# Alternating high and low weight blocks on TensorE, and a router issued in two steps

## The chip, the cores and the metric

The kernel runs on one core of a Trainium2 chip. The metric is the device time of one execution in microseconds. The engines are named as the profile names them: PE (TensorE matmuls), PEld (TensorE weight loads), DVE (VectorE), ACT (ScalarE), POOL (GpSimd), SP (SyncE, which issues most DMAs).

## The reference

Eight sequences of 256 tokens with 1024 features pass through four layers; each layer adds its result to its input. All matrices are 1024 x 1024, and all data are fp32.

```
x = x + L0(x)   # x @ W.T  +  2 * mixture of 8 rank-16 adapters; per token a router picks
                # the top 2 of 8 logits (5.0 is added to one expert per sequence) and
                # weighs them by a softmax over the two
x = x + L1(x)   # x @ W.T + b + coeff[b] * (x @ (2 * mask[b] - 1)),  mask int32, per sequence
x = x + L2(x)   # x @ weight[id[b]].T,  one of 8 full matrices per sequence
x = x + L3(x)   # rank-16 adapter id[b]:  (x @ B[id].T) @ A[id].T
```

## The kernel before

**Precision.** TensorE multiplies fp32r data. A value is split in a high part (a cast to fp32r on ACT) and a low part (the value less its high part, a subtraction on DVE), and a product is taken as high x high + high x low + low x high, in one PSUM accumulator.

**Stages.** The eight sequences are four pairs q, worked on in two halves g of two pairs each. A half is: layer 0 for both its pairs, then layers 1 and 2 of its first pair, then of its second. The work is cut into slots. A half has 16 slots of layer 0 (called s = 0 to 15, with a Strassen-like scheme of seven block products) and 4 x 16 slots of layers 1 and 2.

**Layers 1 and 2.** A slot is one block of 128 output features (m) for one sequence (j): eight k-blocks of weights, each 128 x 128. The activations lie as [k, j, high/low, 256 tokens], so one matmul of the high weight block against 512 columns gives high x high in the first 256 columns and high x low in the last 256; a second matmul of the low weight block against the 256 high columns is added onto the first half. Function `two` (L519) does this: eight high matmuls (L524), then eight low ones (L533). The last slot of all uses `three` instead. `evacuate` later adds the two halves with bias and the residual: ACT copies one half, DVE adds the other.

**Work between the matmuls.** `two` takes three lists of further PE work: `early` runs after the second high matmul, `mid` between the high and the low run, `late` at the end. `main` fills them: layer 3's projections, the rank step and its final matmuls (`proj_pair`, `rank_pair`, `finish` at L463, called through `fill`), and, before the second half begins, the logits of its router.

**Preparation.** ACT casts the high block of the item four ahead (`highs`, L288, five buffers); DVE subtracts for the low block of the item up to three ahead (`lows`, four buffers; line 68 is the helper through which all DVE tensor-tensor operations go). The table `LAGS` delays some of these subtractions around the change from layer 1 to layer 2. Everything is issued in an order written out by hand; each engine works through its own queue in that order.

**Layer 0.** A slot issues, in this order: copies of finished accumulators out of PSUM (`l0_evacuate`, among them L734 in slot 6), casts and subtractions for later slots, the works listed for the slot by `l0_works`, and then the PE work of `l0_main`. The router of a pair runs as such a work: `logits` (L308) and `by_token` (transposes, L319) on PE, then `router` (L323) with some twenty small DVE operations that end in `d`, the difference of the two best logits, an exponential `ex` on ACT (L357), and six small DVE operations that give the two weights; then `expand` (L371) spreads them to `gx`. `gates_by_rank` transposes `gx` on PE (L385) in the middle of a later slot: in slot 3 for the first pair and in slot 6 for the second. In slot 5 the first pair's gates, split into `ghi` and `glo`, enter the products of `lora` (L622) as high x high, high x low and low x high.

In the first half `l0_works` places the router like this:

```
at(2, *both(less, "T1", 1, 0), lambda: router([p0]), lambda: expand(p0))
at(5, lambda: router([p1]), lambda: expand(p1))
```

The second half's router runs for both pairs at once, in the last slot of the first half.

Of the kernel before, what the change touches and what calls it, by code (L numbers as in the profile page):

```python
# [8 lines left out]
F32 = mybir.dt.float32  # L9
# [6 lines left out]
P = 128  # L16
# [3 lines left out]
K = 8  # L20
# [14 lines left out]
def kernel(ctx: ExitStack, tc: tile.TileContext, x, lang, coeff, ids,  # L35
# [23 lines left out]
    gp = ctx.enter_context(tc.tile_pool(name="g", bufs=1))  # L59
# [7 lines left out]
    def tt(o, a, b, op):  # L67
        nc.vector.tensor_tensor(o, a, b, op)  # L68
# [106 lines left out]
    def pair_of(g, j):  # L175
        return 2 * g + 1 - j
# [60 lines left out]
    def fold_quad(t, h, eng=None):  # L237
        for k in range(2):
            c = (2 * h + k) * P
            fold_block(t[:, k, c:c + P], eng)  # L240
# [77 lines left out]
        for n in range(4):  # L318
            nc.tensor.transpose(pts[p][:, n * P:(n + 1) * P], lg[:, n * P:(n + 1) * P], ident)  # L319

    gxs = {}

    def router(pairs):  # L323
        n4 = 4 * len(pairs)
        t = lambda nm, w: gp.tile([P, n4, w], F32, tag=nm, name=nm)
        lv = t("lv", E)
        for i, p in enumerate(pairs):
            quarters = pts.pop(p).rearrange("p (n g e) -> p n e g", n=4, g=4)[:, :, :E, :]
            nc.vector.tensor_reduce(
                lv[:, 4 * i:4 * i + 4].rearrange("p n (e o) -> p n e o", o=1), quarters, AX.X,  # L330
                ALU.add)
        b0, nb = 2 * pairs[0], 2 * len(pairs)
        lv4 = lv.rearrange("p (b h) e -> p b h e", h=2)
        tt(lv4, lv4, bias[:, b0:b0 + nb].rearrange("p b (o e) -> p b o e", o=1)
           .to_broadcast([P, nb, 2, E]), ALU.add)
        revb = rev.to_broadcast([P, n4, E])

        def top(v, nm):
            mx = t(f"mx{nm}", 1)
            nc.vector.tensor_reduce(mx, v, AX.X, ALU.max)  # L340
            eq = t(f"eq{nm}", E)
            tt(eq, v, mx.to_broadcast([P, n4, E]), ALU.is_equal)
            tt(eq, eq, revb, ALU.mult)
            fi = t(f"fi{nm}", 1)
            nc.vector.tensor_reduce(fi, eq, AX.X, ALU.max)
            oh = t(f"oh{nm}", E)
            tt(oh, revb, fi.to_broadcast([P, n4, E]), ALU.is_equal)
            return mx, oh

        m1, oh1 = top(lv, "1")  # L350
        rest = t("rest", E)
        nc.vector.scalar_tensor_tensor(rest, oh1, -3.0e38, lv, ALU.mult, ALU.add)
        m2, oh2 = top(rest, "2")
        d = t("d", 1)
        tt(d, m2, m1, ALU.subtract)
        ex = t("ex", 1)
        nc.scalar.activation(ex, d, AF.Exp)  # L357

        den = t("den", 1)
        nc.vector.tensor_scalar(den, ex, 1.0, 0.5, ALU.add, ALU.mult)  # L360
        wt1 = t("wt1", 1)
        nc.vector.reciprocal(wt1, den)
        wt2 = t("wt2", 1)
        tt(wt2, wt1, ex, ALU.mult)
        tt(oh1, oh1, wt1.to_broadcast([P, n4, E]), ALU.mult)
        tt(oh2, oh2, wt2.to_broadcast([P, n4, E]), ALU.mult)
        tt(oh1, oh1, oh2, ALU.add)
        for i, p in enumerate(pairs):
            gxs[p] = oh1[:, 4 * i:4 * i + 4, :]

    def expand(p):  # L371

        gx = gp.tile([P, 4 * E, R], F32, tag="lg", name=f"gx{p}", bufs=3)
        nc.vector.tensor_copy(gx, gxs[p].rearrange("p n (e o) -> p (n e) o", o=1)
                              .to_broadcast([P, 4 * E, R]))
        gxs[p] = gx
# [21 lines left out]
    def gate(p):  # L398
        tt(gts[p], phs.pop(p), gts[p], ALU.mult)
# [119 lines left out]
    def two(po, hi, lo, xhl, j, early=(), mid=(), late=()):  # L519


        for k in range(K):
            c = slice(k * P, (k + 1) * P)
            mm(po, hi[:, c], xhl[:, k, j].rearrange("p h t -> p (h t)"), start=(k == 0),  # L524
               stop=False)
            if k == 1:
                for f in early:
                    f()
        for f in mid:
            f()  # L530
        for k in range(K):
            c = slice(k * P, (k + 1) * P)
            mm(po[:, :T], lo[:, c], xhl[:, k, j, 0, :], start=False, stop=(k == K - 1))  # L533
        for f in late:
            f()

    def three(po, hi, lo, xhl, j):
        for k in range(K):
# [51 lines left out]
    def link(*args, **kw):  # L590

        mm(*args, skip_group_check=True, **kw)  # L592
# [29 lines left out]
    def lora(p, w):  # L622
        def part(m, o, stop=False):
            hi, lo = gates[p]
            link(o, w[0](m), hi, start=False, stop=False)
            link(o, w[0](m), lo, start=False, stop=False)
            link(o, w[1](m), hi, start=False, stop=stop)
        return part

    def lb_half(i):  # L630
# [16 lines left out]
    def sub(g, o, a, b, h):  # L647
        q = [flat(quad(g, n)[h]) for n in (o, a, b)]
        tt(q[0], q[1], q[2], ALU.subtract)
# [12 lines left out]
    def l0_works(g):  # L662


        p0, p1 = pair_of(g, 0), pair_of(g, 1)
        w = {}

        def at(s, *fs):
            w.setdefault(s, []).extend(fs)

        def add(name, h, src):
            nc.gpsimd.dma_start(quad(g, name)[h], src, accum_op=ALU.add)

        def s1_add(h):
            fold_quad(quad(g, "S1")[h], h)
            add("S1", h, w0[1, 2 + h])

        def s3_add(h):
            t = quad(g, "S3")[h]
            copy(flat(t), flat(quad(g, "S2")[h]))  # L680
            fold_quad(t, h)
            add("S3", h, w0[1, 2 + h])

        def s4_add(h):
            copy(flat(quad(g, "S4")[h]), flat(quad(g, "S2")[h]))
            add("S4", h, w0[0, 2 + h])

        def less(h, name, j, i):

            t = flat(quad(g, name)[h])  # L690
            nc.scalar.mul(t, t, -1.0)  # L691
            add(name, h, x[pair_of(g, j)][:, 4 * i + 2 * h:4 * i + 2 * h + 2])

        def both(f, *args):
            return [lambda h=h: f(h, *args) for h in range(2)]

        def subs(o, a, b):
            return [lambda h=h: sub(g, o, a, b, h) for h in range(2)]

        def lb_parts():  # L700
            copy(lbs[0], lb_raw)
            tt(lbs[1], lb_raw, f32(lbs[0]), ALU.subtract)

        if g == 0:
            at(1, constants, *both(s1_add))
            at(2, *both(less, "T1", 1, 0), lambda: router([p0]), lambda: expand(p0))
            at(3, lb_parts, *subs("S2", "A11", "S1"))
            at(4, *both(s4_add), lambda: gate(p0))
            at(5, lambda: router([p1]), lambda: expand(p1))
        else:  # L710
            at(0, *both(s1_add), *both(less, "T1", 1, 0))
            at(2, lambda: expand(p0))
            at(3, *subs("S2", "A11", "S1"))
            at(4, *both(s4_add), lambda: gate(p0))
            at(5, lambda: expand(p1))
        at(-5, lambda: split_gates(p0, gts[p0]))
        at(4, *both(less, "T3", 1, 1))
        at(7, *subs("T2", "T1", "B22"))
        at(7, *both(s3_add))
        at(8, lambda: gate(p1), lambda: split_gates(p1, gts[p1]), lambda: gate_difference(g))  # L720
        for h in range(2):
            at(9 + h, lambda h=h: add("T4", h, x[p0][:, 4 + 2 * h:6 + 2 * h]))
        for i in range(4):
            at(12 + i, lambda i=i: split_c(p1, i))
        return w
# [183 lines left out]
    def side(n):  # L909

        kind, q, m, j = slots[n]
        if kind == "L1":
            return
        u = pos[slots[n]] % 16
        b = 2 * q
        if q % 2 == 0:
            if u < 2:
                load_l3(b + u)
            if u in (4, 5):
                prep_l3(b + u - 4)  # L920
            if u in (2, 5, 8, 11):
                split_c(q + 1, u // 3)
            return
        l, p = ((9, 10), (11, 12)) if q == 1 else ((4, 5), (9, 10))
        if u in l:
            load_l3(b + u - l[0])
        if u in p:
            prep_l3(b + u - p[0])
        if q == 1:
            if u == 0:  # L930
                X[1] = region(GX[1], "x1", [P, 2, K, N], F32)
            if u in (1, 3, 5, 7):
                k = 4 * (u // 2 % 2)
                load_x(1, u // 4, k, k + 4)
            if u == 10:
                LA[1] = place_la(2)
                nc.sync.dma_start(LA[1], la)
            if u in (12, 13):
                la_parts(1, 4 * (u - 12), 4 * (u - 12) + 4)
            if u == 15:  # L940
                router([2, 3])

    def unit_slot(n):
        kind, q, m, j = slots[n]
# [56 lines left out]
    for h in range(2):  # L1001
        for k in range(2):
            m = 2 * h + k
# [29 lines left out]
    at = l3[b]  # L1033
# [9 lines left out]
    for m in range(0, half, 2):  # L1043
        po = bank(m, f"po{b}_{m}")
        for n in range(2):
            mm(po[:, n * T:(n + 1) * T], at[:, (m + n) * P:(m + n + 1) * P], rt, start=True,
               stop=True)
# [66 lines left out]
```

## Time and profile before

| | |
|---|---|
| median of 3 runs | 614.74 us (613.67 to 614.75) |
| profiled execution, its own time | 613.21 us |
| its span, first to last instruction | 611.0 us |
| mean granted TensorE clock | 0.994 |
| busy: PE, PEld, DVE | 597.0, 500.6, 474.5 us |
| busy: ACT, POOL | 385.1, 140.3 us |
| high matmuls of layers 1 and 2 (L524) | 1016, 392 ns each as recorded |
| low matmuls (L533) | 1016, 283 ns each as recorded |
| bytes moved | 130.22 MB, mean 213 GB/s |

The recorded length of a matmul contains its way through the array and overlaps with the next one; the time that a matmul takes in a row of matmuls is the distance to the next start. Layer 0 of the first half lies at 6 to 119 us, layers 1 and 2 of the first half at 119 to 307, layer 0 of the second half at 307 to 413, layers 1 and 2 of the second half at 413 to 600. Times in the text are microseconds from the span's start unless marked ns.

### The profile page before, as it was taken

How to read it: one execution, taken by the hardware profiler on the slowest of the kernel's cores; microseconds unless marked ns; L12 is line 12 of the kernel's file. 1: busy time of each engine (PE TensorE's matmuls, PEld its weight loads, DVE VectorE, ACT ScalarE, POOL GpSimd, SP SyncE). 2: the span in 40 equal slices, each digit the busy share in tenths (PEclk: the TensorE clock that was granted, in tenths of full speed). 3: DMA queues.
4: the chain of work that ended last, by engine and by line, in shares of the span. 5: the costliest groups of instructions: out<-in, count | busy, mean ns of one | idle time of the engine just before them, and what ended most of it. 6: DMA issues, size and time to landing. Idle time of an engine off the chain costs nothing.

```text
span 611.0 us, 8941 instructions
## 1 busy us (share of the span) xinstructions
PE 597.0 (98%) x3244; PEld 500.6 (82%) x3244; DVE 474.5 (78%) x555; ACT 385.1 (63%) x455; POOL 140.3 (23%) x174
## 2 busy tenths in 40 slices
PE   8997999999999999999999999999999999999995
PEld 7775788888888888888778778888888888888874
DVE  5576858899789999577656776879968999977752
ACT  4574656687678797554544746558866788864431
POOL 0320343014122213122210233511333111511000
PEclk9998999999999999999999999999999999999998
DMA  8986598267685767599940798935767686847404
GB/s 292 330 196 123 137 217 230 104 219 298 191 298 209 248 255 283 183 364 324 291 76 2 163 242 200 276 118 207 276 189 259 207 285 232 301 147 242 173 1 137
DMA packets 39389, 130.22 MB, mean 213 GB/s; under 512 B 4786, under 2 KB 6194, under 8 KB 38578
## 3 DMA queue, kind: packets, MB, share of 16 engines
q1 hardware_dynamic: 34594, 112.62, 52.6%
q0 software_dynamic: 4608, 16.78, 14.9%
q8 instruction: 25, 0.41, 0.3%
q10 hardware_dynamic: 144, 0.26, 0.1%
q14 instruction: 18, 0.15, 0.1%
HBM read 121.25 MB, written 8.39 MB: 212 GB/s over the span
## 4 chain that ended last, share of the span: by engine, by line
PE 92%; DVE 3%; ACT 2%; issue 1%; DMA 1%; ACTq 0%
PE po L524 38%; PE mm L592 27%; PE po L533 20%; PE pl L308 1%; DVE wlo L68 1%; PE pf L463 1%; PE pb L435 1%; ACT x L691 1%; PE ph L619 1%; PE ph L618 1%; PE ph L620 1%; ACT whi L288 1%; DMA x<-in_x 1%; DVE c L68 0%; PE pb L482 0%
## 5 line engine op out<-in xcount | busy, mean ns | idle before, releaser
L524 PE MATMUL po<-hl,whi 128*128 128x512 f32 x1016 | 254.5, 392 | 0.0
L524 PEld LDWEIGHTS po<-hl,whi 128*128 128x128 f32 x1016 | 182.7, 189 | 32.7
L68 DVE TENSOR_TENSOR wlo<-raw,whi 128x1024 fp32r<-128x1024 f32 x128 | 160.9, 1267 | 1.2 <-issue 1.1
L533 PEld LDWEIGHTS po<-hl,wlo 128*128 128x128 f32 x1016 | 137.6, 190 | 11.3 <-issue 1.6
L288 ACT CAST whi<-raw 128x1024 fp32r<-128x1024 f32 x128 | 133.7, 1048 | 18.0 <-PE mm L592 8.4
L533 PE MATMUL po<-hl,wlo 128*128 128x256 f32 x1016 | 142.3, 283 | 0.0
L592 PE MATMUL mm<-whi,whi 128*128 128x512 f32 x224 | 88.9, 397 | 5.1 <-ACT c L734 3.5
L592 PE MATMUL mm<-wlo,whi 128*128 128x512 f32 x224 | 88.2, 394 | 0.0
L235 POOL TENSOR_TENSOR raw<-raw,ident 128x128 f32<-128x128 f32 x72 | 59.2, 823 | 116.9 <-DMA raw<-in_w 86.9
L257 ACT ACTIVATE raw<-raw,negc,c 128x1024 f32<-128x1024 int32 x64 | 79.6, 1243 | 4.2 <-DMA raw<-in_mask 4.2
L592 PE MATMUL mm<-whi,wlo 128*128 128x512 f32 x224 | 71.7, 396 | 0.0
L235 POOL TENSOR_TENSOR w<-w,ident 128x128 f32<-128x128 f32 x28 | 34.6, 1237 | 158.3 <-DMA w<-in_w 134.1
L68 DVE TENSOR_TENSOR raw<-raw,w 128x1024 f32<-128x1024 f32 x56 | 69.3, 1237 | 1.5 <-POOL w L235 0.9
L68 DVE TENSOR_TENSOR wlo<-x,whi 128x1024 fp32r<-128x1024 f32 (+1 forms) x38 | 45.4, 1204 | 21.0 <-issue 10.3
L592 PEld LDWEIGHTS mm<-whi,whi 128*128 128x128 f32 x224 | 42.3, 189 | 17.6 <-ACT c L734 4.0
L592 PEld LDWEIGHTS mm<-whi,wlo 128*128 128x128 f32 x224 | 42.5, 190 | 9.9 <-DVE wlo L68 0.8
L592 PEld LDWEIGHTS mm<-wlo,whi 128*128 128x128 f32 x224 | 42.3, 189 | 8.7
L288 ACT CAST whi<-A 128x1024 fp32r<-128x1024 f32 x26 | 27.3, 1050 | 34.4 <-PE mm L592 16.9
L565 ACT COPY c<-po 128x512 f32<-128x512 f32 (+1 forms) x34 | 18.8, 552 | 47.0 <-PE po L533 47.0
L568 ACT ACTIVATE sum<-po,b_sb 128x512 f32<-128x512 f32 (+1 forms) x36 | 23.1, 642 | 31.6 <-PE po L533 31.6
L288 ACT CAST whi<-x 128x1024 fp32r<-128x1024 f32 x34 | 35.3, 1048 | 8.9 <-PE mm L592 8.9
L68 DVE TENSOR_TENSOR wlo<-A,whi 128x1024 fp32r<-128x1024 f32 (+1 forms) x30 | 35.8, 1193 | 4.7 <-ACT whi L827 2.7
(126 smaller groups left out, 523.6 us busy)
## 6 DMA issues: line engine op xcount, KB each, us to landing
raw<-in_mask SPq DMA_DIRECT2D x64, 512.0 KB, 5.5
raw<-in_w SPq DMA_DIRECT2D x64, 512.0 KB, 4.8
w<-in_w SPq DMA_DIRECT2D x28, 512.0 KB, 3.4
out<-c SPq DMA_DIRECT2D x31, 256.0 KB, 3.0
A<-in_w SPq DMA_DIRECT2D x14, 512.0 KB, 8.1
x<-in_x SPq DMA_DIRECT2D x6, 1024.0 KB, 7.8
A<-in_w POOLq DMA_DIRECT2D x12, 512.0 KB, 7.9
x<-in_x POOLq DMA_DIRECT2D x12, 512.0 KB, 8.5
```

The costliest lines, as they stand in the source:

```text
L68: nc.vector.tensor_tensor(o, a, b, op)
L235: (eng or nc.gpsimd).tensor_tensor(t, t, ident, ALU.add)
L257: nc.scalar.activation(f32(raws[n]), raws[n], AF.Identity, bias=negc[:, b:b + 1], scale=c2[:, b:b + 1])
L288: copy(prep_hi(i), flat(source(i)))
L308: mm(pl[c:c + 32, :], wrs[:, k, :], X[g][:, j, k, :], start=(k < 4), stop=(k >= 4))
L435: mm(pb[c:c + 32, j * T:(j + 1) * T], l3b[b][:, k, :], xts[b][:, k, :], start=(k < 4), stop=(k >= 4))
L463: mm(po[:, i * T:(i + 1) * T], at[:, (m + i) * P:(m + i + 1) * P], rt, start=True, stop=True)
L524: mm(po, hi[:, c], xhl[:, k, j].rearrange("p h t -> p (h t)"), start=(k == 0), stop=False)
L533: mm(po[:, :T], lo[:, c], xhl[:, k, j, 0, :], start=False, stop=(k == K - 1))
L565: copy(xs, po[:, :, T:])
L568: nc.scalar.activation(xs, po[:, :, T:], AF.Identity, bias=b1c)
L592: mm(*args, skip_group_check=True, **kw)
```

## The change

In `two` the low matmul of each k-block now follows the high matmul of the same block; `early` runs after the second pair, `mid` after the fourth pair, `late` after the eighth. The router is cut in two behind `d`: `router` keeps what comes before, and the new `weigh` does the exponential and the weights. In the first half `weigh` and `expand` are issued one slot later than `router`; in the second half `weigh` follows `router` at once. In `lora` the product with the gates' low part comes third instead of second.

```diff
     def router(pairs):
...
         d = t("d", 1)
         tt(d, m2, m1, ALU.subtract)
+        routed[tuple(pairs)] = d, oh1, oh2
+
+    def weigh(pairs):
+
+        n4 = 4 * len(pairs)
+        t = lambda nm, w: gp.tile([P, n4, w], F32, tag=nm, name=nm)
+        d, oh1, oh2 = routed.pop(tuple(pairs))
         ex = t("ex", 1)
         nc.scalar.activation(ex, d, AF.Exp)
...
             mm(po, hi[:, c], xhl[:, k, j].rearrange("p h t -> p (h t)"), start=(k == 0),
                stop=False)
-            if k == 1:
-                for f in early:
-                    f()
-        for f in mid:
-            f()
-        for k in range(K):
-            c = slice(k * P, (k + 1) * P)
             mm(po[:, :T], lo[:, c], xhl[:, k, j, 0, :], start=False, stop=(k == K - 1))
-        for f in late:
-            f()
+            for f in {1: early, 3: mid, K - 1: late}.get(k, ()):
+                f()
...
             link(o, w[0](m), hi, start=False, stop=False)
-            link(o, w[0](m), lo, start=False, stop=False)
-            link(o, w[1](m), hi, start=False, stop=stop)
+            link(o, w[1](m), hi, start=False, stop=False)
+            link(o, w[0](m), lo, start=False, stop=stop)
...
-            at(2, *both(less, "T1", 1, 0), lambda: router([p0]), lambda: expand(p0))
-            at(3, lb_parts, *subs("S2", "A11", "S1"))
+            at(2, *both(less, "T1", 1, 0), lambda: router([p0]))
+            at(3, lambda: weigh([p0]), lambda: expand(p0), lb_parts, *subs("S2", "A11", "S1"))
             at(4, *both(s4_add), lambda: gate(p0))
-            at(5, lambda: router([p1]), lambda: expand(p1))
+            at(5, lambda: router([p1]))
+            at(6, lambda: weigh([p1]), lambda: expand(p1))
...
             if u == 15:
                 router([2, 3])
+                weigh([2, 3])
```

More of the change, by code (lines that the diff above doesn't have):

```diff
@@ L319, in by_token @@
             nc.tensor.transpose(pts[p][:, n * P:(n + 1) * P], lg[:, n * P:(n + 1) * P], ident)
-    gxs = {}
+    gxs, routed = {}, {}
     def router(pairs):
```

## The prediction

> **What bounds the kernel now.** I read first the page's busy shares and its chain of waits, then the waits of PE, then the order of time on PE, ACT and DVE where PE stands still, and last the order of time on PE in the middle of layer 1.
>
> ```profile
> PE 597.0 (98%) x3244; PEld 500.6 (82%) x3244; DVE 474.5 (78%) x555; ACT 385.1 (63%) x455; POOL 140.3 (23%) x174
> PE 92%; DVE 3%; ACT 2%; issue 1%; DMA 1%; ACTq 0%
> PE po L524 38%; PE mm L592 27%; PE po L533 20%; PE pl L308 1%; DVE wlo L68 1%; PE pf L463 1%; PE pb L435 1%; ACT x L691 1%; PE ph L619 1%; PE ph L618 1%; PE ph L620 1%; ACT whi L288 1%; DMA x<-in_x 1%; DVE c L68 0%; PE pb L482 0%
> ```
>
> PE carries 92% of the chain, and the two lines that the change interleaves, L524 (high block) and L533 (low block), are 58% of it. So what counts in layers 1 and 2 is how closely matmuls follow each other, and elsewhere where PE waits. Its waits are few; the largest, in layer 0 of the first half, is explained by four queue entries (PE, ACT, and DVE twice; columns: start, length, engine, line, work, and in brackets the idle time before it and its releaser).
>
> ```profile
> PE mm L592 <- ACT c L734: 3.5, 1, 3.5
> ```
> ```profile
> 48.77 0.39 PE L592 MATMUL mm<-ghi,lb 128*128 128x512 f32 x1
> 52.69 0.50 PE L592 MATMUL mm<-whi,whi 128*128 128x512 f32 x1 [3.53 <-ACT c L734]
> ```
> ```profile
> 51.53 0.20 ACT L357 ACTIVATE ex<-d 128x4 f32<-128x4 f32 x1 [4.09 <-DVE d L68]
> 51.64 1.91 ACT L734 COPY c<-mm 128x1024 f32<-128x1024 f32 x2
> ```
> ```profile
> 51.34 0.15 DVE L68 TENSOR_TENSOR d<-mx,mx 128x4 f32<-128x4 f32 x1
> 52.83 0.43 DVE L374 COPY gx<-oh 128x512 f32<-128x512 f32 x1
> ```
>
> ACT stands 4.09 us at the router's exponential, which needs `d`; the copy that frees the accumulator for slot 6 is queued behind it, and PE waits for the copy.
>
> In layers 1 and 2 PE waits for nothing, and every slot looks like this one (PE's order of time):
>
> ```profile
> 205.51 2.00 PE L524 MATMUL po<-hl,whi 128*128 128x512 f32 x8
> 207.36 1.11 PE L533 MATMUL po<-hl,wlo 128*128 128x256 f32 x8
> 208.31 2.00 PE L524 MATMUL po<-hl,whi 128*128 128x512 f32 x8
> ```
>
> Start to start a slot is 2.79 us: 1.84 for eight high matmuls, 0.95 for eight low ones. The lengths shown overlap, since matmuls are pipelined; I go by starts.
>
> **Part 1: alternation.** It removes and adds no instruction; 127 slots keep 8 + 8 matmuls and their weight loads. The single starts in the trace, averaged over the 110 undisturbed slots, give the steps to the next matmul as 233, 235, 228, 232, 231, 227, 227, 227 ns for the high ones and 113, 119, then six times 120 ns for the low ones: 2793 ns together. Both sizes have a floor, 226.7 and 113.3 ns, exactly two to one as 512 to 256 columns, so the floor is streaming. Above it lie 47 ns in the low run (from the second low matmul on, about 6.7 each) and 26 ns in the first five high ones after it.
>
> No row shows a 512-column and a 256-column matmul taking turns, so I bound the pair. Lower bound: every matmul at its floor, 226.7 + 113.3 = 340 ns, a slot of 2720 ns. For it speaks the one low matmul that follows a high one: it took 113, not 120; its successor's weights were loaded in time, and only back-to-back short matmuls lose. In the alternating order each short matmul is such a first one, and each load for the next short one has 227 ns. Middle: the load for the next high block, under a short matmul, costs the 120 ns of the low run: 226.7 + 120 = 346.7, a slot of 2773. Upper bound: the surcharge that outlives the low run by five high matmuls never dies out: their mean, 232, plus 120 is 352, a slot of 2816. Over the 126 steps: 126 x (2720 - 2793) = -9.2 us, 126 x -20 = -2.5, 126 x 23 = +2.9. I take -9.2, since the row nearest to a lone short matmul is that 113. It is a choice, and the +2.9 stays in the range.
>
> The Trainium skill ("TensorE: Matmul & The Clock Gate", sections "Back-to-back issue gap" and "LDWEIGHTS") speaks against a gain: a matmul of N columns costs N/2.4 + 2.5 ns and a 128-column load 128/1.2 = 107, so a load is just covered by a 256-column matmul (109) in either order, a slot is 8 x (215.8 + 109.2) = 2.60 us (an estimate from that page) both before and after, and the edit is worth nothing. The trace's 2.79 us and its steps of 113 and 120 for the same matmul contradict the rule here, and the measurement decides.
>
> What else alternation moves: the low block is needed one matmul into its slot and no longer 1.84 us into it. By the ends of the subtractions in the trace, DVE has each low block done before its slot begins, by 0.34 us in the tightest (the second slot of a layer 2) and mostly by 3 to 6 us. Shorter slots take 0.07 us from this per slot. I cost it at nothing; if the cover is gone at the four tight places it is up to 0.5 us each. The high buffer is freed at the slot's end, 0.9 us later; casts are done 7 us or more before use, so nothing. The `mid` work runs 0.44 us earlier in its slot. Its inputs come from earlier slots, except in the last but one slot, where `early` makes `pr` and `mid` uses `rt`: L501 starts at 593.06, DVE ends `rt` at 594.20, 1.14 us later; six high matmuls (1.39 us) cover that now, two pairs (0.70 plus 0.12) will not: +0.3 us.
>
> **Part 2: the router in two steps.** Nothing is added, and no DMA changes its place on SP or POOL. The exponential and what hangs on it move behind, on ACT, two casts (and in slot 6 also the two copies of line 734), and on DVE, two subtractions of line 68 at 1.13 us each. For the first pair: `d` is issued at 31.06; two subtractions bring `den` to 33.4, and `den` to the end of `gx` takes 1.5 us as now, so `gx` is ready at 34.9. PE wants it at 34.18 (transposes L385). Today it lies ready at 32.98; so a new wait of 0.8 us. ACT's casts at 39.22 wait for PE, and the ACT work to `ghi` follows on them without a pause, so all up to the second router shifts by 0.8.
>
> For the second pair the 3.53 us wait goes: ACT copies the first accumulator before PE is through with the second, and slot 6 starts as the loras end, at about 49.5. What is late next is `gx`: `d` at 52.2, subtractions until 54.5, `gx` until 56.0. PE has done its 12 matmuls by 52.2 and waits 3.8 us at the transposes, which come at 56.0 instead of 57.13: -1.1 us. The clock is the second half of it:
>
> ```profile
> 53.70:57.10 3.40, 3.40 (x9) 2.54 (x8) 1.92 (x2) 1.74 (x2) 0.00 (x0) 0.50 0.42 82
> ```
>
> In this row by stretches (the 0.50 is the granted clock) half rate follows the stall and makes 12 matmuls last 4.44 us instead of 2.85. A wait of 3.8 us may bring the same after the transposes: +1.6. So layer 0 is worth -1.1 or +0.5; I take the middle, -0.3.
>
> **Part 3: the gates' low part last.** At 46.32 PE waits 0.22 us for `glo`. The new order fills that with a product, but the next thing is the wait for `gx`, which DVE sets: 0. In the other loras the gates are ready in good time.
>
> **Sum.** On the profiled execution, 613.21 us (span 611.0 and 2.2 around it): -9.2 + 0.3 - 0.3 = 604.0. The median of the runs shown, 614.74, lies 1.5 above it, so about 605.5.
>
> **Rivals.** (a) Weight loads bind under the short matmul: 346.7 per pair, 614.74 - 2.5 = 612.2. For it: the steady 120 of the low run. Against: the 113 of its first. (b) Slower: the 6 ns surcharge becomes permanent, 352 per pair, 614.74 + 2.9 = 617.6. For it: five slow high matmuls after each low run, and after the four transposes at 57.13 nine slow ones; in the slots of layer 0 with loras it hardly dies out at all. It decides from 349.1 per pair on, today's mean. (c) The alternation does nothing, as the page's rule has it, and only layer 0 moves: 613.9 (the clock stays full) to 615.5 (it halves).
>
> **How the numbers follow.** Forecast 0.45, (a) 0.17, (b) 0.28, (c) 0.10. The range goes from 603.5 (the forecast with layer 0 at its best, 604.7, and 1.2 less, since the profiled execution lay that far under the median) to 617.8 (rival b), and leaves out some 0.15. Less than 0.2%, 1.2 us, a measurement of this kernel cannot tell from no change. Faster than that are the forecast and (a), 0.62, less 0.02 for (a) with the half clock after the transposes; the same are those 0.02 and (c), 0.12; slower is (b), 0.28. The likeliest case's own range is 603.5 to 608.
>
> **What would show it.** Right: in the order of time of layer 1, alternate matmuls with a slot of about 2.72 us; PE's waits without ACT `c`, but with two for DVE `gx`, near 0.8 and 3.8 us. Wrong: slots of 2.77 (a) or 2.8 and more (b); PE waits for `wlo` at slot starts; no half clock near 57 us, or a longer one.

## The result, and the profile after

The changed kernel took 619.51 us (median of 6, 618.28 to 620.50) beside 614.50 us for the one before (median of 6, 611.54 to 615.94): a ratio of 1.0086, 95% interval 1.0060 to 1.0113. It is slower, by about 5 us, and outside the range that was given. Rival (b), the surcharge that never dies out, had named the place, the sign and nearly the size.

The page after, busy shares and chain, against the lines shown of before:

```profile
PE 600.8 (97%) x3244; PEld 499.8 (81%) x3244; DVE 475.2 (77%) x555; ACT 387.6 (63%) x455; POOL 134.6 (22%) x174
PE 86%; DVE 6%; DMA 3%; ACT 2%; issue 2%; SPq 0%; ACTq 0%; DVEq 0%
PE po L531 39%; PE mm L592 22%; PE po L533 19%; DVE wlo L68 3%; DMA A<-in_w 2%; DMA x<-in_x 1%; PE pf L470 1%; PE pb L442 1%; PE pl L308 1%; DVE x L68 1%; ACT whi L288 1%; DVE c L68 1%; ACT x L691 1%; PE pb L489 0%; PE pg L392 0%
```

The busy shares hide the loss: the work is the same, the share of PE even fell by a point, and the two matmul lines (now L531 and L533) still hold 58% of the chain. One has to look at starts. PE's order of time in the middle of layer 1:

```profile
205.48 0.40 PE L531 MATMUL po<-hl,whi 128*128 128x512 f32 x1
205.71 0.28 PE L533 MATMUL po<-hl,wlo 128*128 128x256 f32 x1
205.83 0.40 PE L531 MATMUL po<-hl,whi 128*128 128x512 f32 x1
206.07 0.28 PE L533 MATMUL po<-hl,wlo 128*128 128x256 f32 x1
206.19 0.40 PE L531 MATMUL po<-hl,whi 128*128 128x512 f32 x1
```

From one high matmul to the next it is 0.35 and 0.36 us. Over the whole of layers 1 and 2 the steps to the next matmul average 235.8 ns after a high matmul and 117.0 after a low one, 353 a pair, in a cycle of three pairs that repeats to within a nanosecond: 232, 118, 241, 120, 235, 114, together 1060 ns. A slot lasts 2.82 or 2.83 us; it was 2.79.

PE's waits, and PE and the two engines behind them in layer 0:

```profile
PE pg L392 <- DVE gx L381: 4.0, 2, 3.6
PE pf L470 <- DVE rt L68: 0.2, 1, 0.2
```
```profile
52.88 0.61 PE L592 MATMUL mm<-whi,wlo 128*128 128x512 f32 x2
57.08 1.12 PE L392 MATMUL pg<-ident,gx 128*128 128x128 f32 x4 [3.58 <-DVE gx L381]
57.84 0.78 PE L592 MATMUL mm<-whi,whi 128*128 128x512 f32 x1
```
```profile
49.41 1.02 ACT L735 COPY c<-mm 128x1024 f32<-128x1024 f32 x1
53.61 0.20 ACT L364 ACTIVATE ex<-d 128x4 f32<-128x4 f32 x1
```
```profile
53.20 0.15 DVE L68 TENSOR_TENSOR d<-mx,mx 128x4 f32<-128x4 f32 x1
53.27 1.22 DVE L68 TENSOR_TENSOR wlo<-x,whi 128x1024 fp32r<-128x1024 f32 x1
54.40 1.22 DVE L68 TENSOR_TENSOR wlo<-A,whi 128x1024 fp32r<-128x1024 f32 x1
56.59 0.43 DVE L381 COPY gx<-oh 128x512 f32<-128x512 f32 x1
```

The wait of 3.5 us for the copy has become one of 3.58 us for `gx`: the copy now runs 4 us ahead of the exponential, but two subtractions run between `d` and the rest of the router. The granted clock (last but two of the columns) is halved from about the end of this wait on, as it was behind the old one:

```profile
56.70:60.10 3.40, 3.02 (x9) 2.58 (x10) 0.32 (x1) 0.59 (x1) 0.00 (x0) 0.50 0.04 7
```

Where the time went, by the starts of the stages in the two profiled executions (spans 611.0 and 616.4):

| stage | before, us | after, us | difference |
|---|---|---|---|
| layer 0, first half | 112.79 | 114.38 | +1.59 |
| layers 1 and 2, first half | 189.24 | 190.94 | +1.70 |
| layer 0, second half | 104.69 | 104.70 | +0.01 |
| layers 1 and 2, second half | 187.15 | 189.47 | +2.32 |
| last matmul of layer 2 to the end | 10.98 | 10.97 | -0.01 |

So +4.0 us lie in layers 1 and 2. Of the +1.59 in layer 0, +1.07 lie before the first logits matmul, where no instruction has moved: that stretch was 10.9 us before and 12.0 after (0.73 of it one wait for a cast on ACT), and between 10.7 and 12.3 in the kernels below that begin like the old one. Since it varies that much among kernels that begin alike, I do not count it as an effect of the change. The router's own share is +0.5.

### The profile page after: what moved, and what is told of

Same layout as the page of the kernel before. It is cut to its first block, busy times and chain, and to the rows that moved or that the text cites. A ratio compares the mean times of both kernels' runs of the same rounds, so it can differ in the third digit from the quotient of the medians.

```text
span 616.4 us, 8939 instructions
## 1 busy us (share of the span) xinstructions
PE 600.8 (97%) x3244; PEld 499.8 (81%) x3244; DVE 475.2 (77%) x555; ACT 387.6 (63%) x455; POOL 134.6 (22%) x174
## 4 chain that ended last, share of the span: by engine, by line
PE 86%; DVE 6%; DMA 3%; ACT 2%; issue 2%; SPq 0%; ACTq 0%; DVEq 0%
PE po L531 39%; PE mm L592 22%; PE po L533 19%; DVE wlo L68 3%; DMA A<-in_w 2%; DMA x<-in_x 1%; PE pf L470 1%; PE pb L442 1%; PE pl L308 1%; DVE x L68 1%; ACT whi L288 1%; DVE c L68 1%; ACT x L691 1%; PE pb L489 0%; PE pg L392 0%
## 5 line engine op out<-in xcount | busy, mean ns | idle before, releaser
L531 PE MATMUL po<-hl,whi 128*128 128x512 f32 x1016 | 359.9, 399 | 0.0
L533 PE MATMUL po<-hl,wlo 128*128 128x256 f32 x1016 | 285.2, 281 | 0.0
L531 PEld LDWEIGHTS po<-hl,whi 128*128 128x128 f32 x1016 | 190.8, 188 | 48.9 <-issue 2.5
L533 PEld LDWEIGHTS po<-hl,wlo 128*128 128x128 f32 x1016 | 191.9, 189 | 0.2
L235 POOL TENSOR_TENSOR w<-w,ident 128x128 f32<-128x128 f32 x28 | 31.4, 1121 | 165.2 <-DMA w<-in_w 103.2
L68 DVE TENSOR_TENSOR c<-po,c 128x512 f32<-128x512 f32 (+1 forms) x36 | 23.4, 652 | 21.1 <-ACT c L565 19.9
```

Of the source, the lines that this page charges most:

```text
L235: (eng or nc.gpsimd).tensor_tensor(t, t, ident, ALU.add)
```

## The experiments

### The parts taken one by one

**e1_alternate_only**: before, with the new `two` alone (the diff's hunk on `two`).

> Before, with only the alternation in `two`. Theory A (the alternation costs, because a surcharge of some 6 ns per matmul never dies out): high steps near 236 ns and low steps near 117 as in the changed kernel, a slot of 2.82 to 2.83 us, and +4 us on the whole (126 slots times 0.03 us), so about 618.5 beside 614.5. Rival B (the changed kernel's extra time is from the router and not from the alternation): a slot as long, but the total within 1 us of before, which would mean that the time lost in the slots was slack elsewhere.

Measured: 618.52 us (617.40 to 621.28) beside 614.01, ratio 1.0080 (1.0052 to 1.0109). High steps are 236.0 ns and low steps 116.8 on average over layers 1 and 2, slots of 2.82 and 2.83 us; layers 1 and 2 took 190.94 and 189.47 us, as in the changed kernel. Theory A holds, rival B falls: the alternation alone carries the loss.

**e2_router_only**: the changed kernel with the old `two`.

> The changed kernel with the old order in `two`: only the router in two steps and the gates' low part last. Theory A: PE waits for gx twice, some 0.5 and 3.6 us, the wait of 3.5 us for the copy goes, half the clock comes for 3.4 us near 57 us as before; the first slot of layer 1 is within 0.6 us of before when the start is taken off, total 614.5 to 615.5. Rival B: the router is the main loss, total near 618.

Measured: 614.55 us (613.19 to 616.32) beside 614.01, ratio 1.0015 (0.9998 to 1.0033): no difference that the interval tells from none. PE waited 4.3 us for `gx` in two waits, 3.6 the longer, and the clock was halved from 56.0 to 59.5 us. A wait and a stretch at half clock were replaced by another wait and another stretch at half clock.

### Why a lone short matmul is not at its floor

e5, e7, e8 and e13 to e17 are e1 with the further edit that is shown. These kernels, and e3 and e4, were run once each, and only the steps in that one trace are read.

**e5_low_full_width**: no short matmul at all.

```diff
-            mm(po[:, :T], lo[:, c], xhl[:, k, j, 0, :], start=False, stop=(k == K - 1))
+            mm(po, lo[:, c], xhl[:, k, j].rearrange("p h t -> p (h t)"), start=False,
+               stop=(k == K - 1))
```

> Alternation only, but the low block is multiplied with all 512 columns (low x low is computed too and lands in the second half of the accumulator), so there is no short matmul, while high and low blocks still take turns. Theory A1 (the short matmul causes the surcharge): all steps at the floor of 226.7 ns, 16 of them 3.63 us a slot. Rival A2 (the turn from one weight tile to the other causes it): steps of 233 to 236, 3.73 us a slot.

Measured: every step of layer 1 is 226 or 227 ns, a slot 3.63 us. PE's order of time:

```profile
205.24 0.39 PE L526 MATMUL po<-hl,wlo 128*128 128x512 f32 x1
205.47 0.39 PE L524 MATMUL po<-hl,whi 128*128 128x512 f32 x1
205.70 0.39 PE L526 MATMUL po<-hl,wlo 128*128 128x512 f32 x1
205.92 0.39 PE L524 MATMUL po<-hl,whi 128*128 128x512 f32 x1
```

Taking turns between two weight tiles costs nothing when both matmuls have 512 columns; with the 256-column matmul in between it does.

**e7_low_narrow** and **e8_high_narrow** halve one of the two weight loads, by leaving out half of the products of the narrowed blocks.

```diff
+            n = P if k in (0, K - 1) else 64            # e7
+            c2 = slice(k * P, k * P + n)
-            mm(po[:, :T], lo[:, c], xhl[:, k, j, 0, :], start=False, stop=(k == K - 1))
+            mm(po[:n, :T], lo[:, c2], xhl[:, k, j, 0, :], start=False, stop=(k == K - 1))
...
+            n = 64 if k else P                          # e8
+            c2 = slice(k * P, k * P + n)
-            mm(po, hi[:, c], xhl[:, k, j].rearrange("p h t -> p (h t)"), start=(k == 0),
+            mm(po[:n], hi[:, c2], xhl[:, k, j].rearrange("p h t -> p (h t)"), start=(k == 0),
                stop=False)
```

> Alternation only, and the low blocks of k = 1 to 6 are cut to 64 stationary columns, so half of their products are left out. The load that runs under a long matmul is halved, the load of the next high block, under the short matmul, stays at 128 columns. Theory L (the load under the short matmul sets the surcharge): a pair stays near 353 ns. Theory S (every load adds to it, or the turns between the blocks do): a pair between 340 and 349.

> Alternation only, and the high blocks of k = 1 to 7 are cut to 64 stationary columns, so half of their products are left out. The load under the short matmul is halved, the load under the long one stays at 128 columns. Theory L (the load under the short matmul sets the surcharge): steps at the floor, 226.7 and 113.3, a pair of 340 ns and a slot of 2.72 us. Rival D (it is not the load but the short matmul as such, say the rate at which PE issues): a pair stays near 353.

Measured: e7 231.8 + 117.4 = 349.2 ns a pair, a slot of 2.79 us; e8 227.8 + 113.8 = 341.6 ns a pair, a slot of 2.73 us, with the surcharge left only around the one full-width high block of each slot. PE's order of time in e8:

```profile
204.53 0.39 PE L526 MATMUL po<-hl,whi 128*64 128x512 f32 x1
204.76 0.28 PE L528 MATMUL po<-hl,wlo 128*128 128x256 f32 x1
204.87 0.39 PE L526 MATMUL po<-hl,whi 128*64 128x512 f32 x1
205.10 0.28 PE L528 MATMUL po<-hl,wlo 128*128 128x256 f32 x1
```

Of the 13 ns that a pair pays above 340, the load of the next high block, the one under the short matmul, accounts for some 12, and the load under the long one for some 4 (the two overlap). That spoke for theory L: a load not covered by a 113 ns matmul. But a narrowed block also writes only 64 rows of its result, and these two runs do not tell that from the shorter load. The next three runs tested theory L with a longer cover.

**e13_low_272**, **e14_low_288**, **e15_low_320**: the low matmul a little longer.

```diff
-            mm(po[:, :T], lo[:, c], xhl[:, k, j, 0, :], start=False, stop=(k == K - 1))
+            mm(po[:, :272], lo[:, c], xhl[:, k, j].rearrange("p h t -> p (h t)")[:, :272],
+               start=False, stop=(k == K - 1))           # 272, 288 or 320
```

> Alternation only, with the low block multiplied by 272 columns instead of 256 (16 columns of low x low are computed too). Theory L (the next high block's load, about 120 ns, is not covered by a 113 ns matmul): floors are 226.7 and 120.4 ns, the load is just covered, a pair of 347 to 350 ns, less than the 353 of 256 columns although more is computed. Rival D (the surcharge of 6.7 ns per matmul belongs to the taking of turns): 353 + 7 = 360.

> As e13_low_272 with 288 columns. Theory L: floors 226.7 + 127.5 = 354 a pair, the surcharge gone. Rival D: 367.

> As e13_low_272 with 320 columns. Theory L: floors 226.7 + 141.7 = 368 a pair, steps even. Rival D: 381.

Measured, high + low step: 234.6 + 125.4 = 360 ns with 272 columns, 232.1 + 131.3 = 363 with 288, 233 + 147 = 380 with 320. PE's order of time in e15:

```profile
205.50 0.31 PE L526 MATMUL po<-hl,wlo 128*128 128x320 f32 x1
205.65 0.40 PE L524 MATMUL po<-hl,whi 128*128 128x512 f32 x1
205.88 0.31 PE L526 MATMUL po<-hl,wlo 128*128 128x320 f32 x1
206.03 0.40 PE L524 MATMUL po<-hl,whi 128*128 128x512 f32 x1
```

Theory L had 347 to 350, 354 and 368, rival D 360, 367 and 381. Theory L fell: with 147 ns of cover the high steps still read 233. Rival D met 272 and 320 columns and missed 288 by 4 ns. My floors are in doubt too: 5/8 of 226.7 would be 142 ns for 320 columns, and the step was 147.

**e16_all_384** and **e17_low_384**: equal and unequal lengths.

```diff
+            n = 2 * T if k == 0 else 384                 # e16; in e17 the high one stays at 512
-            mm(po, hi[:, c], xhl[:, k, j].rearrange("p h t -> p (h t)"), start=(k == 0),
+            mm(po[:, :n], hi[:, c], xhl[:, k, j].rearrange("p h t -> p (h t)")[:, :n],
...
+            mm(po[:, :384], lo[:, c], xhl[:, k, j].rearrange("p h t -> p (h t)")[:, :384],
```

> Alternation only, with 384 columns in the low matmul and in the high ones of k = 1 to 7 (a third of the high x low products is left out, some low x low is added): as many columns per pair as 512 + 256, in equal parts. If the surcharge comes from turns of unequal length: even steps near 170 to 173 ns, a pair of 340 to 347. If it comes from the closeness of loads or from short matmuls in general: more than 350 a pair.

> Alternation only, with 384 columns in the low matmul and 512 in the high one. If unequal length is what costs: the high steps stay at 233 and the pair near 404 to 407. If a load needs a certain length of cover, which 384 columns give: steps of 227 and 170 to 173, a pair of 397 to 400.

Measured: with 384 in both, steps of 173 and 174 ns, 347 a pair, disturbed only beside the one 512 of each slot. With 512 and 384, 231.6 + 175.0 = 407 a pair. PE's order of time in e16 (behind the 512 at 205.59) and then in e17:

```profile
205.82 0.34 PE L527 MATMUL po<-hl,wlo 128*128 128x384 f32 x1
206.00 0.34 PE L525 MATMUL po<-hl,whi 128*128 128x384 f32 x1
206.18 0.34 PE L527 MATMUL po<-hl,wlo 128*128 128x384 f32 x1
```
```profile
205.71 0.34 PE L526 MATMUL po<-hl,wlo 128*128 128x384 f32 x1
205.88 0.39 PE L524 MATMUL po<-hl,whi 128*128 128x512 f32 x1
206.12 0.34 PE L526 MATMUL po<-hl,wlo 128*128 128x384 f32 x1
206.29 0.40 PE L524 MATMUL po<-hl,whi 128*128 128x512 f32 x1
```

Beside the steps of rows of equal length, 173.5 and 226.7, a pair of 512 and 384 pays 6.4 ns more, most of it in the long matmul (4.9), although the load of its block has 175 ns of cover. So in these runs the surcharge goes with turns of unequal length (e1, e13 to e15, e17) and not with turns of equal length (e5, e16), and it goes away when the high block is narrow (e8). What in PE ties the two together no run here shows; that stays open.

**e3_groups_of_2** and **e4_groups_of_4**: high and low in shorter runs (early and mid after the matching group).

```diff
+        for k0 in range(0, K, 2):                        # e3; 4 in e4
+            for k in range(k0, k0 + 2):
                 ... high block k
+            for k in range(k0, k0 + 2):
                 ... low block k
```

> Old router. Two high matmuls, then two low ones, four times a slot. If the surcharge lives on in the long matmuls until five have passed: 4 x (233 + 235 + 113 + 119) = 2.80 us a slot, between the 2.79 of runs of eight and the 2.83 of the alternation. If it is a price per short matmul that follows a short one, and nothing else: 4 x (227 + 227 + 113 + 119) = 2.74.

> Old router. Four high matmuls, then four low ones, twice a slot (mid runs after the first four of each). If the surcharge lives on: 2 x (233 + 235 + 228 + 232 + 113 + 119 + 120 + 120) = 2.80 us a slot. If it is only a price per short matmul that follows a short one: 2 x (4 x 227 + 113 + 119 + 120 + 120) = 2.76.

Measured: groups of two 2.79 us a slot (233, 233, 115, 116 ns), groups of four 2.81. Both lie well above the 2.74 and 2.76 of a price that falls on short matmuls alone: high steps average 232 to 233 in both groupings. Runs of eight, at 2.79, are as good as any grouping tried.

### What the two waits in layer 0 are worth

**e6_gates_at_end**: old `two`; the second pair's weights first thing behind the copies in slot 6, its transposes at the slot's end. Diff against the changed kernel, without the hunk on `two`:

```diff
-            at(2, *both(less, "T1", 1, 0), lambda: router([p0]))
-            at(3, lambda: weigh([p0]), lambda: expand(p0), lb_parts, *subs("S2", "A11", "S1"))
+            at(2, *both(less, "T1", 1, 0), lambda: router([p0]), lambda: weigh([p0]),
+               lambda: expand(p0))
+            at(3, lb_parts, *subs("S2", "A11", "S1"))
...
-            at(6, lambda: weigh([p1]), lambda: expand(p1))
+            at(-6, lambda: weigh([p1]), lambda: expand(p1))
...
-                    6: lambda: gates_by_rank(p1)}
+                    -6: lambda: gates_by_rank(p1)}
```

> Old order in `two`. The router of the first pair is whole again as before; for the second pair weigh and expand go to the start of slot 6, behind the copies of the accumulator and ahead of the casts and subtractions, and the transposes of gx go from the middle of slot 6 to its end; low gates last. If the two waits are what layer 0 loses: no PE wait for the copy and none for gx, no half clock near 57 us, slot 6 through at about 55 instead of 60.3, and 4.5 to 5 us off the total, about 609.5. Rival: what comes next in layer 0 (a DMA add or a subtraction on DVE for slots 7 to 9) waits instead, and 2 us or less is left.

Measured: 608.15 us (607.88 to 608.23) beside 614.01, ratio 0.9896 (0.9879 to 0.9912), the fastest kernel of this study and faster than both. No wait for the copy on ACT or for `gx`, no half clock between the first matmuls and the last 4 us of the span; layer 0 of the first half took 107.65 us instead of 112.79. What comes next does wait, as the rival had it, but only 1.2 us: PE waits for DVE's additions `c` at the start of slot 8. PE's order of time:

```profile
53.55 0.62 PE L599 MATMUL mm<-whi,wlo 128*128 128x512 f32 x2
54.01 0.60 PE L392 MATMUL pg<-ident,gx 128*128 128x128 f32 x4
54.37 0.48 PE L599 MATMUL mm<-whi,whi 128*128 128x512 f32 x1
```

**e9_weigh_first** has the first two of e6's three pieces above, **e10_transposes_late** only the last one (on the changed router, old `two`).

> As e6_gates_at_end, but the transposes of gx stay in the middle of slot 6: only the place of weigh and expand differs from the router of before. The copies no longer stand behind the exponential, and gx is ready near 53.0, as in e6, while PE comes to the transposes near 51.7: one wait of about 1.3 us, no half clock, total 609.5. If the place of the transposes is what matters instead, the wait stays near 3.5 us and the total near 614.

> As e2_router_only (the changed router order, old order in `two`), but the transposes of gx go to the end of slot 6. gx stays as late as in e2 (end near 56.5), PE comes to the end of slot 6 near 55: a wait of 1.5 to 2 us in place of 3.6, too short for half the clock, and the wait of 0.5 us for the first pair stays. Total 610 to 611. If only the place of weigh matters, the total stays at 614.5.

Measured: e9 610.28 us, ratio 0.9942 (0.9925 to 0.9960), one wait for `gx` of 1.67 us; e10 610.56 us, ratio 0.9958 (0.9941 to 0.9975), two waits of together 1.6 us. In neither was the clock halved in layer 0. Each half does most of the work: it takes off some 2 us of waiting, and with it the half clock, which had cost 1.6 us.

**e11_alternate_and_gates**: e6 with the new `two`.

> e6_gates_at_end with the alternation put back. If the two costs add up, the slots are 2.82 to 2.83 us and the total 608.2 + 4.0 = 612.2. If they share a cause, less than 2 us is added.

Measured: 613.28 us, ratio to before 0.9991 (0.9972 to 1.0010), slots of 2.82 and 2.83 us: 5.1 us above e6's median where 4.0 was expected. In the profiled executions layers 1 and 2 take 4.0 us more than in e6, and 1.07 us more lie ahead of the first logits matmul, the stretch that varies. The two parts add up; the alternation takes back nearly all that the better router gives.

**e12_copy_before_subs**: e6, and two DVE subtractions moved behind the emptying of an accumulator.

```diff
-        at(7, *subs("T2", "T1", "B22"))
+        at(-8, *subs("T2", "T1", "B22"))
```

> e6_gates_at_end, and the two subtractions that make T2 are issued in slot 8 behind the additions that empty the accumulator, no longer in slot 7 ahead of them. PE's wait of 1.2 us at the start of slot 8 and the one of 0.4 us in the second half should go: 606.6. Rival: the casts that need T2 come late for slot 10, PE waits there, total 608 or more.

Measured: 612.23 us, ratio to before 0.9974 (0.9954 to 0.9993), where e6 took 608.15. PE's waits:

```profile
PE mm L599 <- ACT ghi L401: 3.3, 2, 1.7
PE pt L319 <- ACT lg L312: 1.4, 1, 1.4
```

The waits for the additions on DVE (1.2 and 0.4 us in e6) went, but the subtractions now push back the gates' split (`ghi`), and PE waits for that in slot 9 of both halves, 3.3 us together. The rival had the sign and not the place. Behind the 1.4 us before the second half's router stands a late transfer: the copies of the logits (`lg`) are queued on ACT behind a cast that waits for `c<-in_la`, in e12 (first row) until 296.54 us and in e6 (second row) until 293.47:

```profile
296.54 0.62 ACT L651 CAST laghi<-c 128x512 fp32r<-128x512 f32 x1 [2.73 <-DMA c<-in_la]
293.47 0.62 ACT L651 CAST laghi<-c 128x512 fp32r<-128x512 f32 x1 [1.45 <-DMA c<-in_la]
```

SP issued that transfer at 283.45 in e12 and 283.47 in e6. Why it landed 3 us later in e12 is open; PE's wait for `lg` stands in e2, e3, e7 and e8 as well (0.3 to 2.2 us), so it need not come from this edit.

## Why the prediction was wrong

**The step that failed** is the choice in part 1: "I take -9.2, since the row nearest to a lone short matmul is that 113." The upper bound, 352 ns a pair and +2.9 us, came nearest; measured were 353 ns and +4.0. The 113 ns row was read as a property of a lone short matmul, but it stood behind eight long ones; with one long matmul before each, the low steps run from 113 to 120 ns. The row that mattered stood beside it: the first high matmul after a low run, at 233 ns, and four more slow ones, which a shortage of loads hardly explains, since the low run gets through one load every 120 ns. The prediction named these rows, as the rival's, and gave them the smaller chance. e8 shows pairs at both floors, 227 and 113 ns, where the high block is narrow; e1 shows that with full blocks the alternation does not reach them (236.0 and 116.8).

The floors themselves were less than they seemed. Seven of eight low matmuls took 119 to 120 ns in the kernel before, and 384 columns took 173.5 ns (e16) where "exactly two to one" would make them 170: "so the floor is streaming" did not hold.

**The rule of the Trainium skill** that was weighed there ("TensorE: Matmul & The Clock Gate", section "Back-to-back issue gap"), as the prediction applied it, gave no effect of the order; e1 shows one of 0.8%. Its N/2.4 + 2.5 ns, which the section calls the gap of an isolated matmul, would make the steps 215.8 and 109.2 ns (an estimate from that page). Here rows of equal matmuls took 226.7 and 120 ns a step.

**Part 2** was nearly right in each term and chosen wrongly at the end. Predicted waits of 0.8 and 3.8 us for `gx`; the bracketed idle times are 0.42 and 3.58, and by starts the first one moved PE by 0.58. From the first logits to the second pair's transposes the prediction gave -1.1 us; it was -0.92 (39.12 instead of 40.04). The half clock was left open at +1.6; from the transposes to layer 1 it was +1.44 (63.26 instead of 61.82). Net +0.5, the upper of the two ends, where the middle was taken. Here waits of 3.5 and 3.6 us brought half the clock, for 3.4 us in most runs and for 6.8 in e5 and e7, and the 1.67 us of e9 did not. The same page (section "Part 1: The HAM clock gate") has the clock halved after an idle window of about 3.4 us, which agrees.

The top of the range, 617.8, had no room for the surcharge and the half clock together. With the measured terms the sum is 614.5 + 4.0 + 0.5 = 619.0 beside 619.51.

**Part 3** (0) and the last slot (+0.3) held: PE's waits no longer list `glo`, and a wait of 0.2 us for `rt` is new. The cover of the low blocks held as well: no wait for `wlo` appears in layers 1 and 2.

**Rival (a)**, 346.7 a pair, occurs: behind the slots with layer 3's short matmuls in the first half, the alternation runs for four slots at 230 + 117 ns, 2.77 us a slot. The same instructions have two steady rhythms, and the slower is the usual one.

## What to carry to other kernels

A step at its floor once, behind a particular history, is no evidence for a steady rhythm: before interleaving matmuls of different lengths, look at how the long ones behave after the short ones, and reckon with their slow steps becoming permanent. When a wait is moved away by splitting a chain, follow the chain's other end through every queue: here the copy came free, and two subtractions of 1.1 us that slipped into the chain cost the same wait, and the same half clock, a few matmuls later. Placing the chain's second half ahead of those subtractions, and its consumer half a slot later, brought 6 us.

## What the runs showed of the hardware

In rows of fp32r matmuls of equal length, each with a full 128 x 128 load, the step is 226.7 ns for 512 columns (e5), 173.5 for 384 (e16) and 120.0 for 256 (the low runs of the kernel before, from the third on). The three lie on one line, 53.5 and 53.2 ns for 128 columns. Only beside narrow blocks (e8) do 256-column matmuls keep to 113 ns; elsewhere that step comes singly.

Against the sum of these steps a pair of unequal lengths in turn costs 6 to 7 ns more: 512 with 256 (e1: 353 beside 346.7) and with 384 (e17: 407 beside 400.2), and by an estimate along the line also with 272 (e13: 360 beside 353.4) and 320 (e15: 380 beside 373.4). It does not always: with 288 (e14) it is 3 ns, and in the other rhythm of the alternation, 347 a pair, nothing.
